# A graph attention layer with q in two float32r pieces and a new cut of the edges into six parts

## The chip, the cores and the metric

One NeuronCore of a Trainium2 chip runs the whole kernel. The metric is the device time of one execution in microseconds. The engines are named as in the profile: PE is the matrix engine (PEld its weight loads), DVE is VectorE, ACT is ScalarE, POOL is GpSimd, SP is SyncE.

## The reference

12,500 nodes with 128 features, 412,500 edges with 64 features. The list `dst` is sorted (it plays the role of the attention's target), `src` is not. Per edge an attention score is made from q of the source, k of the target and the edge's features; a softmax over all edges weighs v of the target, which is summed by source.

```python
h, q, k, v = (x @ W + b for W, b in ((Wn, bn), (Wq, bq), (Wk, bk), (Wv, bv)))
eh = edge_features @ We + be
attn_in = concatenate([q[src], k[tgt], eh], axis=-1)
hmid = leaky_relu(attn_in @ A1 + b1, 0.2)
scores = leaky_relu(hmid @ A2 + b2, 0.2)          # 8 heads
w = softmax(scores.mean(axis=-1), axis=0)         # over all edges
out = segment_sum(w[:, None] * v[tgt], src)
y = layernorm(h + out) * gamma + beta
result = layernorm(x + y)
```

## The kernel before, in words

The edges come in 403 groups of 8 tiles of 128 edges. The groups are cut into six parts (`CUTS`). The nodes are 98 blocks of 128 rows; an edge belongs to the block of its source.

**Making records.** `make(p)` goes through the groups of part p. For a group it loads the edge features and a window of the k and v table, builds one-hots on VectorE (`onehots`, `masked`, `places`: L823 to L883), multiplies them on the matrix engine into a record of 256 numbers per edge (`rows`: L901, L907), copies the records from PSUM on ScalarE (`evacuate`: L918, L919, into a tile `rec` of four times 128 edges, six of them in the pool `rp`), and scatters each 128 edges with an indirect DMA from GpSimd (L930) to the place in `rtab` that is the next free one of the edge's block. Eight scatters per group, 3,224 in all. When a part's last group has been counted, `ended` makes its mask (L967). Each part has its own number of tiles per block, wide enough for the blocks' counts (`plan.tiles`): 5, 6, 7, 7, 7, 7 in the kernel before. Rows of `rtab` that may stay without a record are filled with zeros by DMAs (`fill`, `fill_top`) while the first three parts are made.

**Using records.** A unit is two blocks of one part: 10, 12 or 14 tiles. 49 units a part, 294 in all, 3,822 tiles. For a unit, `load` fetches its records (`rt`), `load_q` its q rows (`qs`), `sources`, `turn`, `turned`, `put`, `spread` bring each edge's row number within its block across all partitions (`sl`, `slT`, `row`, `rowB`). Then come chunks of up to four tiles: `onehot` builds the one-hot `ohT` of a chunk (L1122), `hidden` transposes the record's first half into PSUM (L1133) and adds q by one matmul per piece of q and block (L1142: a chunk that spans two blocks is split in two), `sloped` and `leaky` finish the hidden layer (L1153, L1157). `scores` and `heads` (L1170, L1196) give the scores of the unit, `maximum` (L1217) its running reference, `weights` the exponentials; `select` and `weigh` (L1244, L1258) build weighted one-hots in f32, and `add` (L1287) sums v by source. Sums of a part are added to those of the part before in `atab`.

A planner (`sums_of`) gives each of these calls a step; a unit takes eight steps, also with three chunks, while `e` is 1. The order of the instructions is fixed: while part p is made, the steps of part p - 1 are spread evenly between its groups, from the first load of a part to the first load of the next. Part 0 is made beside the making of the tables (`tables`), the last part's steps run alone after all records are made, and `closing` does the two norms.

**q.** `tables` computes q and h for 14 groups of seven blocks. `parts3` splits q into three bf16 pieces whose sum holds f32's precision (a copy on ScalarE, a difference on VectorE, and so on: L1526, L1531), which lie in `qtab` in DRAM, 768 bytes a row.

Of the kernel before, what the change touches and what calls it, by code (L numbers as in the profile page):

```python
# [11 lines left out]
BF = mybir.dt.bfloat16  # L12
I32 = mybir.dt.int32
# [7 lines left out]
P = 128  # L21
D = 128
# [11 lines left out]
CUTS = 0, 0.1266, 0.2804, 0.4615, 0.6427, 0.8238, 1  # L34
# [9 lines left out]
class Plan:  # L44
# [4 lines left out]
    def __init__(self, n, e, nb, groups):  # L49
        self.n, self.e, self.nb, self.groups = n, e, nb, groups  # L50
        cut = [round(groups * c) for c in CUTS]
# [401 lines left out]
def sorted_path(  # L453
# [17 lines left out]
    qtab = dram.tile([P, nb, 3 * D], BF, name="qtab")  # L471
# [274 lines left out]
    rp = pool("rec", 6)  # L746
# [280 lines left out]
    def sums_of(bp):  # L1027
# [3 lines left out]
        for p, bs, t in units:  # L1031
            nt = len(bs) * t
            nk = -(-nt // 4)
            L, e = 2 * nk, int(nk > 3 or p < NP - 1)
            turn = (11 if nk > 3 else 12) if e else 8
            if plans:
                s0 += 2 * plans[-1][1] if not plans[-1][5] else max(8, 2 * plans[-1][1])


            load_at = free[-BLKS] + 1 if len(free) >= BLKS else 0  # L1040
            lead = turn + 8 if p in starts or p == 0 else turn + 8 + LATE
            s0 = max(s0, load_at + lead - 1)
# [29 lines left out]
        def load_q(i):  # L1072
            bs = units[i][1]
            qs = qp.tile([P, 2, 3, D], BF, name="qs")
            nc.sync.dma_start(
                out=qs[:, : len(bs), :, :].rearrange("p b s d -> p b (s d)"),
# [42 lines left out]
        def onehot(i, t0, n, k):  # L1119
            st = state[i]  # L1120
            st["oh"][k] = op_.tile([P, 4 * P], BF, name="ohT")
# [6 lines left out]
        def hidden(i, t0, c, n, k):  # L1128
# [9 lines left out]
            while j0 < t0 + n:  # L1138
                j1 = min(t0 + n, (j0 // t + 1) * t)
                cols = slice((j0 - t0) * P, (j1 - t0) * P)  # L1140
                for s in range(3):
                    nc.tensor.matmul(  # L1142
                        ph[:, cols], st["qs"][:, j0 // t, s, :], oh[:, cols], start=False,
                        stop=(s == 2 and j1 == t0 + n),
# [389 lines left out]

    def tables():
# [13 lines left out]
        for i, (kv, g) in enumerate(jobs):  # L1549
# [25 lines left out]
            else:  # L1575
                sq = sp.rearrange("p b s t d -> p (b s t d)")[:, : NB * 3 * D].rearrange(
                    "p (b s o d) -> p b s o d", b=NB, s=3, o=1
                )
                yield from parts3([sq[:, :, s, :, :] for s in range(3)], ns[:, :, 0:1, :], 1)
# [153 lines left out]
```

## Time and profile before

| | |
|---|---|
| median of three runs | 5045.82 us (5041.39 to 5046.07) |
| the profiled execution | 5048.47 us, its span 5046.7 us |
| mean granted clock of the matrix engine | 0.909 |
| PE, DVE, ACT, POOL busy | 81%, 81%, 65%, 66% of the span |
| DMA | 1505 MB, 298 GB/s |

A row of a group reads: line, engine, operation, written tile from read tiles, shape, count, then busy time and the mean ns of one, then the idle time of the engine just before them and what ended most of it. A row of stretches reads: from:to, length, then busy time and count of each engine shown, the granted clock of the matrix engine, the DMA engines' busy share, GB/s. A row of waits reads: engine and line, what it waited for, us in total, times, the longest.

### The profile page before, as it was taken

Reading aid. Unit: us, or ns where it says so; the run is one execution under the profiler, and the core shown is the slowest. Engines: PE = TensorE matmul, PEld = TensorE weight load, DVE = VectorE, ACT = ScalarE, POOL = GpSimd, SP = SyncE. Lnnn points to the kernel's source line nnn. Section 1 sums busy time; section 2 is a strip of 40 time slices with the busy share of each in tenths; the row PEclk is TensorE's granted clock in tenths of the full one; section 3 lists DMA queues with packets and bytes.
Section 4 is the critical chain, followed back from the end, with each engine's and each line's share of the span. In section 5 each row is a group of like instructions: output and inputs, shape, how many; then the busy total and the mean of one; then the engine's idle time right before and its main releaser. Section 6 shows DMA issues by size and latency. Waiting matters only on the chain.

```text
span 5046.7 us, 95840 instructions
## 1 busy us (share of the span) xinstructions
PE 4086.8 (81%) x31427; PEld 3042.3 (60%) x31870; DVE 4082.6 (81%) x9078; ACT 3271.6 (65%) x8487; POOL 3318.5 (66%) x3267
## 2 busy tenths in 40 slices
PE   3566667888888888898889899989899999888980
PEld 2333445566666665676667676666676667667760
DVE  7888867778888887888888898888798889666668
ACT  2443345566666666677767777777677777777886
POOL 3777777677777777777777777777777777310002
PEclk6777678899999999999999999999999999999995
DMA  5899889998899988899989899889898999787763
GB/s 179 306 314 354 302 276 335 335 313 292 296 327 329 338 304 288 285 324 318 310 301 316 291 326 317 313 308 311 299 318 311 323 315 325 259 283 271 252 230 140
DMA packets 616624, 1505.35 MB, mean 298 GB/s; under 512 B 104462, under 2 KB 329889, under 8 KB 614324
## 3 DMA queue, kind: packets, MB, share of 16 engines
q1 hardware_dynamic: 461024, 1069.73, 64.1%
q0 software_dynamic: 154752, 429.39, 22.3%
q8 instruction: 253, 4.15, 0.3%
q14 instruction: 255, 2.09, 0.1%
q10 hardware_dynamic: 340, 0.01, 0.0%
HBM read 929.49 MB, written 608.37 MB: 305 GB/s over the span
## 4 chain that ended last, share of the span: by engine, by line
DMA 39%; DVE 24%; PE 11%; POOL 9%; ACT 8%; issue 7%; SPq 1%; DVEq 0%; ACTq 0%; POOLq 0%
DMA rtab<-rec,idx 16%; POOL rtab L930 9%; DMA row<-slT 8%; DMA rt<-rtab 6%; DMA rowB<-row 6%; DVE ohd L844 3%; DVE hm L1157 3%; ACT ohw L1258 3%; PE psm L1287 2%; DVE few L834 2%; ACT rec L918 2%; DVE pos L881 2%; PE pkv L907 2%; DVE ohT L1122 2%; PE psc L1170 1%
## 5 line engine op out<-in xcount | busy, mean ns | idle before, releaser
L930 POOL DMA_INDIRECT rtab<-rec,idx x3224 | 3256.1, 1010 | 1086.1 <-issue 790.7
L918 ACT ACTIVATE rec<-pkv 128x1024 f32<-128x1024 f32 x806 | 822.0, 1020 | 1029.0 <-PE pkv L907 620.2
L1258 ACT ACTIVATE ohw<-ohs,w 128x128 f32<-128x128 bf16 x3822 | 1261.1, 399 | 203.2 <-DVE ohs L1244 84.6
L1287 PE MATMUL psm<-rt,ohw 128*128 128x128 f32 x7644 | 1113.4, 288 | 0.6 <-ACT ohw L1258 0.6
L1287 PEld LDWEIGHTS psm<-rt,ohw 128*128 128x128 f32 x7644 | 985.5, 198 | 75.9 <-ACT hm L1153 10.1
L1157 DVE TENSOR_TENSOR hm<-ph,hm 128x512 f32<-128x512 f32 (+1 forms) x1078 | 669.9, 621 | 271.3 <-ACT hm L1153 263.5
L1133 PE MATMUL ph<-ident,rt 128*128 128x128 f32 x3822 | 648.1, 288 | 154.3 <-DVE hm L1157 150.5
L1142 PE MATMUL ph<-ohT,qs 128*128 128x512 bf16 (+3 forms) x3673 | 719.4, 312 | 35.5 <-DVE ohT L1122 8.9
L901 PE MATMUL pkv<-kvs,ohd 128*128 128x256 bf16 x3224 | 528.7, 290 | 174.2 <-ACT rec L918 153.3
L1133 PEld LDWEIGHTS ph<-ident,rt 128*128 128x128 f32 x3822 | 423.0, 145 | 382.5 <-issue 180.0
L907 PE MATMUL pkv<-WeS,eat 64*128 64x128 f32 x6448 | 626.1, 317 | 0.0
L1122 DVE TENSOR_SCALAR ohT<-rowB,iotaP 128x512 bf16<-128x512 uint8 (+1 forms) x1078 | 499.5, 463 | 152.3 <-DMA rowB<-row 152.1
L1153 ACT ACTIVATE hm<-ph 128x512 f32<-128x512 f32 (+1 forms) x1078 | 577.8, 536 | 57.2 <-PE ph L1142 47.1
L907 PEld LDWEIGHTS pkv<-WeS,eat 64*128 64x128 f32 x6448 | 462.4, 202 | 189.7 <-issue 183.9
L844 DVE TENSOR_SCALAR ohd<-dstb,node 128x1152 bf16<-128x1152 uint8 x404 | 564.9, 1399 | 4.3 <-DMA dstb<-dtab 4.3
L901 PEld LDWEIGHTS <-ohd 128*128 128x128 bf16 x3224 | 314.5, 104 | 379.2 <-issue 289.5
L1142 PEld LDWEIGHTS <-qs 128*128 128x128 bf16 x4116 | 394.8, 99 | 140.6 <-issue 18.6
L1244 DVE TENSOR_TENSOR ohs<-iotaE,sl 128x512 bf16<-128x512 bf16 (+1 forms) x1078 | 419.1, 389 | 4.2 <-ACT ohw L1258 4.2
L834 DVE TENSOR_REDUCE few<-oh 128x99 bf16<-128x792 bf16 x403 | 395.1, 980 | 13.9
L870 DVE TENSOR_TENSOR ats<-pc,oh 128x792 f32<-128x792 f32 x403 | 391.2, 971 | 16.5 <-PE pc L852 16.1
L881 DVE TENSOR_REDUCE pos<-ats 128x8 f32<-128x792 f32 x403 | 389.6, 967 | 1.7
L1170 PE MATMUL psc<-hm,A2s 128*32 128x512 f32 (+3 forms) x2352 | 343.3, 552 | 55.4 <-DVE slT L1101 52.4
(157 smaller groups left out, 3700.6 us busy)
## 6 DMA issues: line engine op xcount, KB each, us to landing
rt<-rtab SPq DMA_DIRECT2D x196, 1820.0 KB
eat<-in_ea SPq DMA_DIRECT2D x201, 512.0 KB
rt<-rtab SPq DMA_DIRECT2D x49, 1560.0 KB
rt<-rtab SPq DMA_DIRECT2D x49, 1300.0 KB
qs<-qtab SPq DMA_DIRECT2D x294, 192.0 KB
rtab<-rec,idx POOLq DMA_INDIRECT x3224
dstb<-dtab SPq DMA_DIRECT2D x201, 256.0 KB
rtab<-empty SPq DMA_DIRECT2D x98, 520.0 KB
```

The costliest lines, as they stand in the source:

```text
L844: nc.vector.tensor_scalar(to, ids[:, cols], node, None, op0=ALU.is_equal)
L901: nc.tensor.matmul(pk[:, h, i, :], ohd[t], kvs, start=(i == 0), stop=False,)
L907: nc.tensor.matmul(pk[:, h, i, :D], eat[h * DE : (h + 1) * DE, (j + i) * P : (j + i + 1) * P], WeS[h * DE : (h + 1) * DE, :], start=False, ...
L918: nc.scalar.activation(rec[:, :, :, : 2 * D], pk, AF.Copy)
L930: one_tile = nc.gpsimd.indirect_dma_start(out=rtab[p % TABS][:, :], out_offset=bass.IndirectOffsetOnAxis(ap=idxs[g][:, t : t + 1], axis=0) ...
L1122: nc.vector.tensor_scalar(st["oh"][k][:, : n * P], st["rowB"][:, t0 * P : (t0 + n) * P], iotaP, None, op0=ALU.is_equal,)
L1133: nc.tensor.matmul(ph[:, j * P : (j + 1) * P], st["rt"][:, t0 + j, :D], ident, is_transpose=True, start=(j == 0), stop=False,)
L1142: nc.tensor.matmul(ph[:, cols], st["qs"][:, j0 // t, s, :], oh[:, cols], start=False, stop=(s == 2 and j1 == t0 + n),)
L1153: nc.scalar.activation(hm, state[i]["ph", k][:, : n * P], AF.Copy, scale=SLOPE)
L1157: nc.vector.tensor_tensor(hm, ph[:, : n * P], hm, op=ALU.max)
L1258: nc.scalar.activation(ohw[:, j, :], ohs[:, :, j], AF.Copy, scale=st["w"][:, t0 + j : t0 + j + 1])
L1287: nc.tensor.matmul(st["psS"][:, (1 + u) * P : (2 + u) * P], ohw[:, j, :], st["rt"][:, t0 + j, D : 2 * D], start=(k == 0), stop=(k == t - 1),)
```

## The change

q is kept as two pieces of four bytes instead of three of two bytes. The first is q as ScalarE writes it in the type float32r, the second the difference to q; `qtab` has 1,024 bytes a row. The one-hot `ohT` is written in float32r too, and `hidden` issues two matmuls per segment instead of three, both operands float32r. In the built program such a matmul stands without a weight load of its own, as f32 ones do; a bf16 one has a separate load. The six parts have 62, 73, 73, 73, 62 and 60 groups (before: 51, 62, 73, 73, 73, 71), which gives 6, 7, 7, 7, 6 and 6 tiles per block. The number of units and of tiles stays (294 and 3,822); the chunks go from 1,078 to 1,029, the q matmuls from 4,116 (1,372 segments of three) to 2,646 (1,323 of two). The block tiles filled with zeros go from 980 to 632. The pool of `rec` has five tiles instead of six. The threshold in `e` moves so that the last part, now with three chunks a unit, keeps its eight steps.

```diff
+FR = mybir.dt.float32r
-CUTS = 0, 0.1266, 0.2804, 0.4615, 0.6427, 0.8238, 1
+CUTS = 0, 62, 135, 208, 281, 343
-        cut = [round(groups * c) for c in CUTS]
+        cut = [groups * c // 403 for c in CUTS] + [groups]
-    qtab = dram.tile([P, nb, 3 * D], BF, name="qtab")
+    qtab = dram.tile([P, nb, 2 * D], FP, name="qtab")
-    rp = pool("rec", 6)
+    rp = pool("rec", 5)
-            L, e = 2 * nk, int(nk > 3 or p < NP - 1)
+            L, e = 2 * nk, int(nk > 2 or p < NP - 1)
-            qs = qp.tile([P, 2, 3, D], BF, name="qs")
+            qs = qp.tile([P, 2, 2, D], FR, name="qs")
-            st["oh"][k] = op_.tile([P, 4 * P], BF, name="ohT")
+            st["oh"][k] = op_.tile([P, 4 * P], FR, name="ohT")
-                for s in range(3):
+                for s in range(2):
                     nc.tensor.matmul(
                         ph[:, cols], st["qs"][:, j0 // t, s, :], oh[:, cols], start=False,
-                        stop=(s == 2 and j1 == t0 + n),
+                        stop=(s == 1 and j1 == t0 + n),
                     )
+    def parts2(to, q):
+        yield
+        nc.scalar.activation(to[:, :, 0, :, :].bitcast(FR), q, AF.Copy)
+        yield
+        yield
+        nc.vector.tensor_tensor(to[:, :, 1, :, :], q, to[:, :, 0, :, :], op=ALU.subtract)
+        yield
+        yield
-                yield from parts3([sq[:, :, s, :, :] for s in range(3)], ns[:, :, 0:1, :], 1)
+                yield from parts2(sq, ns[:, :, 0:1, :])
```

More of the change, by code (lines that the diff above doesn't have):

```diff
@@ L1073, in load_q @@
             bs = units[i][1]
-            qs = qp.tile([P, 2, 3, D], BF, name="qs")
+            qs = qp.tile([P, 2, 2, D], FR, name="qs")
             nc.sync.dma_start(
-                out=qs[:, : len(bs), :, :].rearrange("p b s d -> p b (s d)"),
+                out=qs[:, : len(bs), :, :].rearrange("p b s d -> p b (s d)").bitcast(FP),
                 in_=qtab[:, bs[0] : bs[-1] + 1, :],
@@ L1575, in tables @@
             else:
-                sq = sp.rearrange("p b s t d -> p (b s t d)")[:, : NB * 3 * D].rearrange(
-                    "p (b s o d) -> p b s o d", b=NB, s=3, o=1
-                )
-                yield from parts3([sq[:, :, s, :, :] for s in range(3)], ns[:, :, 0:1, :], 1)
+                sq = sp.rearrange("p b s t d -> p (b s t d)").bitcast(FP)[
+                    :, : NB * 2 * D
+                ].rearrange("p (b s o d) -> p b s o d", b=NB, s=2, o=1)
+                yield from parts2(sq, ns[:, :, 0:1, :])
                 bl = slice(g * NB, (g + 1) * NB)
```

## The prediction

> **What bounds the kernel now.** I read the page's header first, then GpSimd's scatter line (L930) by stretch, then who holds ScalarE up, then the matrix engine's timeline at the end. The stretches are cut where each part's mask is made (L967, the instruction that closes a part): about 622, 1301, 2047, 2815, 3576 and 4322 us.
>
> ```profile
> span 5046.7 us, 95840 instructions
> PE 4086.8 (81%) x31427; PEld 3042.3 (60%) x31870; DVE 4082.6 (81%) x9078; ACT 3271.6 (65%) x8487; POOL 3318.5 (66%) x3267
> ...
> L967 DVE TENSOR_TENSOR mask<-placed,high x6: 659/862/864, 622.2 to 4321.8; 128x686 bf16<-128x686 f32 x4, 128x490 bf16<-128x490 f32 x1, 128x588 bf16<-128x588 f32 x1
> ...
> L930 POOL DMA_INDIRECT rtab<-rec,idx x371 | 406.8, 1097 | 119.8 <-issue 93.9 <-ACT rec L919 7.9 <-DMA rtab<-rec,idx 6.4
> L930 POOL DMA_INDIRECT rtab<-rec,idx x504 | 498.9, 990 | 180.9 <-issue 120.2 <-ACT rec L919 21.0 <-DMA rtab<-rec,idx 9.8
> L930 POOL DMA_INDIRECT rtab<-rec,idx x585 | 583.5, 997 | 178.3 <-issue 145.7 <-DMA rtab<-rec,idx 11.0 <-ACT ohw L1258 5.5
> L930 POOL DMA_INDIRECT rtab<-rec,idx x571 | 572.5, 1003 | 174.1 <-issue 136.5 <-ACT ohw L1258 11.6 <-DMA rtab<-rec,idx 6.4
> ...
> 3582.05 0.96 POOL L930 DMA_INDIRECT rtab<-rec,idx  x1 [0.31 <-issue]
> 3583.32 0.96 POOL L930 DMA_INDIRECT rtab<-rec,idx  x1 [0.30 <-issue]
> 3584.59 0.96 POOL L930 DMA_INDIRECT rtab<-rec,idx  x1 [0.30 <-issue]
> ```
>
> The header makes GpSimd look idle a third of the time. The L930 rows (stretches 97:622, 622:1301, 2815:3576, 3576:4322) say otherwise. In 2815:3576, 585 scatters of 0.997 us, each behind 178.3/585 = 0.305 us of idle time, fill 761.8 of 761 us. The three timeline rows show the same beat: one scatter every 1.27 us, idle time 0.30 us without a cause outside GpSimd. So from the third part on GpSimd issues scatters without a break, and a group of 1,024 edges (8 scatters) takes 10.42 us whatever the other engines do. Until 4322 us the kernel is a scatter generator; only the end, when no records are made any more, belongs to the others.
>
> How close are the others behind? The waits of ScalarE tell, for 2815:3576 and for 3576:4322:
>
> ```profile
> ACT rec L918 <- DMA rtab<-rec,idx: 105.6, 56, 3.7
> ...
> ACT rec L918 <- PE pkv L907: 91.8, 60, 5.6
> ...
> L1287 PE MATMUL psm<-rt,ohw 128*128 128x128 f32 x7644 | 1113.4, 288 | 0.6 <-ACT ohw L1258 0.6
> 2815.00:3576.00 761.00, 199.79 (x1374) 176.03 (x1373) 0.97 0.90 312
> 3576.00:4322.00 746.00, 201.69 (x1384) 176.80 (x1383) 0.97 0.90 312
> 4322.00:4907.00 585.00, 212.11 (x1532) 194.13 (x1532) 0.98 0.75 256
> 4907.00:5047.00 140.00, 0.00 (x0) 0.00 (x0) 0.52 0.43 161
> ```
>
> In the first of the two stretches ScalarE stood 105.6 us because all `rec` buffers were still with GpSimd: slack. In the second its largest wait is for the matrix engine's next record. L1287 has two records a tile, so its windows count tiles: 687 tiles over 73 groups (9.4 a group) with slack, 692 over 71 (9.75 a group) with next to none, while GpSimd still never starved. So 9.75 tiles a group is the point where the two loads balance. The last two rows give the end: 766 tiles in 585 us without groups (0.764 us a tile), then 140 us of norms.
>
> Is that end bound by the matrix engine? One steady unit of 14 tiles there:
>
> ```profile
> 4700.32 1.06 PE L1287 MATMUL psm<-rt,ohw 128*128 128x128 f32 x8
> ...
> 4702.30 0.38 PE L1217 MATMUL psm<-ident,mx 128*128 128x128 f32 x2
> 4702.52 1.06 PE L1287 MATMUL psm<-rt,ohw 128*128 128x128 f32 x8
> 4703.51 1.06 PE L1170 MATMUL psc<-hm,A2s 128*32 128x512 f32 x8
> 4704.50 0.66 PE L1133 MATMUL ph<-ident,rt 128*128 128x128 f32 x4
> 4704.99 0.82 PE L1142 MATMUL ph<-ohT,qs 128*128 128x384 bf16 x6
> 4705.65 0.66 PE L1287 MATMUL psm<-rt,ohw 128*128 128x128 f32 x4
> 4706.15 0.60 PE L1133 MATMUL ph<-ident,rt 128*128 128x128 f32 x4
> 4706.58 0.81 PE L1142 MATMUL ph<-ohT,qs 128*128 128x512 bf16 x3
> 4707.23 1.05 PE L1287 MATMUL psm<-rt,ohw 128*128 128x128 f32 x8
> 4708.12 0.95 PE L1196 MATMUL psm<-headsum,z 128*128 128x4 f32 x8
> 4709.00 0.22 PE L1094 MATMUL psc<-identB,sl 128*14 128x128 bf16 x1
> 4709.15 0.44 PE L1133 MATMUL ph<-ident,rt 128*128 128x128 f32 x2
> 4709.43 0.49 PE L1142 MATMUL ph<-ohT,qs 128*128 128x256 bf16 x3
> 4709.76 0.50 PE L1287 MATMUL psm<-rt,ohw 128*128 128x128 f32 x3
> ```
>
> No gap stands in these rows: yes. From 4700.32 to 4709.76 a unit takes 9.44 us. Taken start to start, the q matmuls (L1142) are 0.65 for a full chunk of 512 columns in three pieces (4706.58 to 4707.23), the same for the other (4700.32 to 4702.30 is 0.89 of L1287, 0.43 of L1133 and the rest), 0.66 for the chunk split 384+128, 0.33 for 256: 2.29 us.
>
> **The change, term by term.** *The cuts.* 403 groups and 3,224 scatters stay, at GpSimd's beat, so moving groups between parts costs nothing in itself; the six parts come to 6, 7, 7, 7, 6, 6 tiles a block in place of 5, 6, 7, 7, 7, 7 (3,822 tiles in both). The end now belongs to a part of 6 tiles. Of its 766 tiles 686 are the last part's; at 12 tiles a unit in place of 14 it has 766 x 12/14 = 657, in the same 54.7 units. Price of a 12-tile unit: from 9.44 take q (2.29), the turn (0.15), the maximum (0.22), heads (0.88) and scores (0.99): 4.91 us over 14 tiles, 0.351 each. So 12 x 0.351 = 4.21, plus 0.15, 0.22, 3/4 of heads (0.66) and of scores (0.74): 5.98 without q.
>
> *q in two pieces.* A 12-tile unit has chunks 512, 256+256, 512: with three bf16 pieces 2 x 0.65 + 2 x 0.33 = 1.96 us. The trace has no float32r matmul. Ends: a bf16 piece, 0.65/3 = 0.22 us per 512 columns, and an f32 one (L1287: two records a tile, four tiles from 4707.23 to 4708.12, 0.22 us per 128 columns), four times as much. I take the lower: the two f32 records are what carries 24 bits of mantissa, and a type whose one piece falls short of that, so that q needs two, should have no second record. That is an inference, and the middle, one record at the spacing of the single f32 record (L1133, 0.43 us for four of 128 columns, twice bf16), is a rival below. So two thirds: 1.31 us, a unit of 7.29 us; 2.29 becomes 1.53 in a 14-tile unit, 0.76 less.
>
> ```profile
> L1142 PEld LDWEIGHTS <-qs 128*128 128x128 bf16 x4116 | 394.8, 99 | 140.6 <-issue 18.6
> L1133 PEld LDWEIGHTS ph<-ident,rt 128*128 128x128 f32 x3822 | 423.0, 145 | 382.5 <-issue 180.0 <-DVE hm L1157 149.3 <-PE psm L1287 9.6
> ```
>
> Against this change speaks a rule of the Trainium skill ("TensorE: Matmul & The Clock Gate", Weight-path perf modes): the fast weight load is on for types other than FP32. The trace agrees in kind: a bf16 weight load took 99 ns, an f32 one 145 ns. By that page's figure for a plain load (its section on LDWEIGHTS: columns over 1.2 GHz, so an estimate of 0.107 us) a piece of 128 columns would take 0.107 in place of 0.054 us; the 12-tile units have none, the fifth part's units two each, 49 x 2 x 0.053 = 5 us, and the sum would be 4972.
>
> *The end.* 54.7 units at 9.44 are 516 of the 585 us; the other 69 are DMA waits early in it:
>
> ```profile
> DVE ohT L1122 <- DMA rowB<-row: 93.3, 43, 4.3
> DVE sl L1086 <- DMA rt<-rtab: 77.6, 46, 15.5
> ```
>
> These stay. 54.7 x 7.29 + 69 = 468; since units follow each other faster than loads used to, I add 12 (0 to 25): 480 us in place of 585. The 140 us behind it stay.
>
> *What the cuts take back.* While the fifth part is made (62 groups), the fourth part's 686 tiles are worked off: 11.06 tiles a group, 1.31 over the balance of 9.75. At 9.44/14 = 0.674 us a tile that is 0.88 us a group, at 0.764 it is 1.00; two-piece q gives back 49 x 0.76/62 = 0.60. So 0.28 to 0.40 a group over the beat, 17 to 25 us; I take 24, as no slack was left there. In the sixth (60 groups, some 600 tiles, 10.0 a group) 0.17 more against 49 x 0.65/60 = 0.53 less: nothing.
>
> *Five `rec` buffers.* A buffer is four scatters, 5.1 us of cover for GpSimd. In the middle parts ScalarE waits for buffers, so cover is spare; where a part ends a dip of up to one buffer may starve GpSimd: 0 to 5 x 5.1 = 25, I take 8.
>
> *The one-hot in 4 bytes.*
>
> ```profile
> L1122 DVE TENSOR_SCALAR ohT<-rowB,iotaP 128x512 bf16<-128x512 uint8 x833 | 409.8, 492 | 152.3 <-DMA rowB<-row 152.1
> L1122 DVE TENSOR_SCALAR ohT<-rowB,iotaP 128x256 bf16<-128x256 uint8 x245 | 89.7, 366 | 0.0
> L1157 DVE TENSOR_TENSOR hm<-ph,hm 128x512 f32<-128x512 f32 x833 | 569.4, 684 | 217.6 <-ACT hm L1153 212.6 <-ACT ohw L1258 3.7
> ```
>
> 256 more columns cost 126 ns, two elements a nanosecond. With f32 output it is between 492 and L1157's 684 ns; the source stays one byte, so I take 492. At 684, 49 x 3.5 x 0.19 = 33 us of VectorE a part, of which the crowded fifth might show half.
>
> *Tables and fills.* q's two pieces save one ScalarE and one VectorE pass a block group in part 0, where nobody waits for them (GpSimd's beat). Of 980 block tiles of empty rows 632 remain. In 97:622 a scatter took 1.097 us against 1.003 later, 371 x 0.094 = 35 us lost to crowded queues; I take 6 off, 0 to 17. qs loads grow by a third (192 KB each), beside work.
>
> *Sum.* 4322 - 6 + 24 + 8 + 480 + 140 = 4968 of span; the profiled execution took 5048.5 us for its span of 5046.7, and is 2.7 over the median of 5045.8. So 4967 us, 1.6% faster. A step of 0.2% (10 us) is about what a measurement of this kernel can tell.
>
> **The rivals.** *Two float32r pieces cost as much as three bf16* (0.17). Then a unit is 7.94 us, the end 515 with the same 12; the fifth part is 0.88 to 1.00 a group over the beat, 54 to 62; sum 4322 - 6 + 58 + 8 + 515 + 140 - 1 = 5036, between 5000 and 5085. For it: only 4-byte rows slower than bf16 are in the trace.
>
> *The matrix engine becomes the bound* (0.16): one record a piece, but at twice bf16's spacing, as L1133. Two pieces then cost 4/3 of three: 2.61 in a 12-tile unit (8.59 us), 3.05 in a 14-tile one, 0.76 more. The fifth part is over its beat by 0.94 + 0.60 = 1.54 a group, 95 us; the sixth by 0.17 + 0.53 = 0.70, 42; the third and fourth use up their slack and lose some 10 each; the end is 551. Sum 4322 - 6 + 95 + 42 + 20 + 8 + 551 + 140 - 1 = 5171. It turns slower than before once two pieces cost over some 1.03 times what three do. At L1287's full f32 price it would be hundreds more. Against: the inference above.
>
> *Cover lost* (0.05): `rec` with five and a 4-byte one-hot at 684 ns starve GpSimd through the last three parts, 25 + 3 x 17: about 5035.
>
> **How the numbers follow.** The forecast has 0.62; its own range is 4912 (no giving back, all of the fills' gain, 468 at the end) to 5005. With the first rival up to 5060 some 0.8 is held. Faster: 0.61 of the forecast, 0.10 of the first rival, 0.02 of the last; within 10 us 0.05; slower the second rival and 0.06 of the others.
>
> **What would show it.** Right: scatters still 1.27 us apart through the third and fourth part; L1142 two records a segment, 0.43 us a full chunk start to start; first gaps of GpSimd behind `rec` in the fifth part; last mask near 4350; some 480 us from there to the last L1287; norms 140. Wrong: gaps of GpSimd in every part (cover), L1142 at 0.65 us or more a chunk (price), or an end that waits for `rt` and `rowB` instead of the matrix engine.

## The result and the profile after

The changed kernel takes 5081.92 us (median of five runs, 5072.5 to 5090.75) where the kernel before takes 5045.13 in the same session: a ratio of 1.0072, 95% interval 1.006 to 1.0084. It is slower by 37 us, 0.7%; the forecast was 4967, faster by 79, with a range of its own up to 5005 and up to 5060 with the first rival's.

The page's header after, the line that closes a part (its six times run from the first to the last part's end), and the stretches cut at those times, in the columns of the prediction:

```profile
span 5085.8 us, 92648 instructions
...
L968 DVE TENSOR_TENSOR mask<-placed,high x6: 760/834/864, 721.7 to 4394.5; 128x588 bf16<-128x588 f32 x3, 128x686 bf16<-128x686 f32 x3
...
2248.00:3011.00 763.00, 680.72 (x5383) 533.48 (x5383) 660.49 (x1427) 555.09 (x1469) 584.90 (x585) 0.95 0.91 316
3011.00:3734.00 723.00, 645.31 (x5084) 508.95 (x5083) 606.63 (x1353) 530.64 (x1418) 506.09 (x508) 0.95 0.90 310
3734.00:4395.00 661.00, 579.13 (x4644) 440.15 (x4643) 563.68 (x1223) 457.21 (x1256) 477.86 (x482) 0.96 0.90 311
4395.00:4947.00 552.00, 468.78 (x3257) 380.16 (x3256) 310.59 (x924) 350.44 (x1083) 33.77 (x19) 0.91 0.71 245
4947.00:5086.00 139.00, 0.00 (x0) 0.00 (x0) 118.32 (x550) 84.12 (x224) 29.00 (x14) 0.50 0.45 168
```

The ledger, from these cuts and those of before. After 281 groups the changed kernel stands at 3011; the kernel before reached group 281 at about 2815 + 22 x 10.42 = 3044. So it is **33 us ahead** there. From then on before needed 1277 us for 122 groups, 10.47 each. The fifth part (62 groups) took 723 us where that beat gives 649: **74 lost**. The sixth (60 groups) took 661 for 628: **32 lost**. The end took 552 for 585: **32 won**, where 105 were forecast. The norms took 139 for 140. In all 39 us of span, which is the 5085.8 against 5046.7.

The mask that closes a part is VectorE's, and it can come before GpSimd has sent the part's last records. So the same ledger was taken at GpSimd's scatters, counted in the two traces. The changed kernel is 15 us ahead after 62 groups, 39 after 135 and 38 after 281; the next 62 groups lose 68, the last 60 lose 25. The last scatter comes at 4345 before and at 4400 after, the first load of the last part's records right behind it (4347 and 4403). Before, the last mask stood 23 us ahead of that scatter, after it only 5. From that first load to the last L1287 the 49 units of the last part took 559 us before and 544 after: of the 32 us won at the end by the masks, only 15 belong to the smaller units.

GpSimd's scatter line in the second, the fifth and the sixth part (722:1483, 3011:3734, 3734:4395):

```profile
L931 POOL DMA_INDIRECT rtab<-rec,idx x588 | 583.0, 991 | 179.2 <-issue 146.3 <-DMA rtab<-rec,idx 10.7 <-ACT ohw L1259 4.6
L931 POOL DMA_INDIRECT rtab<-rec,idx x508 | 507.1, 998 | 217.2 <-issue 116.4 <-ACT rec L920 27.4 <-ACT w L1236 18.5
L931 POOL DMA_INDIRECT rtab<-rec,idx x482 | 478.4, 993 | 183.4 <-issue 114.6 <-ACT rec L920 24.3 <-ACT ohw L1259 12.8
```

In the second part the idle time before a scatter is 179.2/588 = 0.305 us, the beat. Before it was 180.9/504 = 0.359 there: the old second part, with 62 groups beside units of 10 tiles, had been starved, and the new one with 73 beside 12 is not. By the beat, this cost the kernel before 679 - 62 x 10.42 = 33 us, as much as the lead at 281 groups. In the fifth part the idle time is 0.428, in the sixth 0.380, and ScalarE's `rec` stands among the causes: the groups now wait for something else.

The q matmuls of full chunks, the one-hot, and the q matmuls' weight loads (before: 492 ns a one-hot, 99 ns a weight load); then the weight loads of `add` in the kernel before:

```profile
L1143 PE MATMUL ph<-ohT,qs 128*128 128x512 f32 x1176 | 437.5, 454 | 0.0
L1123 DVE TENSOR_SCALAR ohT<-rowB,iotaP 128x512 fp32r<-128x512 uint8 x882 | 430.9, 489 | 100.5 <-DMA rowB<-row 100.1
L1143 PEld LDWEIGHTS ph<-ohT,qs 128*128 128x128 f32 x2646 | 411.1, 197 | 15.5 <-DVE ohT L1123 15.0
...
L1287 PEld LDWEIGHTS psm<-rt,ohw 128*128 128x128 f32 x7644 | 985.5, 198 | 75.9 <-ACT hm L1153 10.1 <-issue 7.8 <-ACT ohw L1258 7.7
```

The records name the type f32, but there is one record a piece (1176 = 2 x 588 full chunks), as the forecast inferred; what grew is the weight load, 197 ns for 99. The rule of the Trainium skill that the prediction weighed ("TensorE: Matmul & The Clock Gate", Weight-path perf modes) agrees in kind, but not in size: the page's figure gave an estimate of 0.107 us a load, the trace has 0.197. The prediction charged it to the split chunks alone, 5 us. The trace before had a nearer price: the f32 loads of L1287 took 198 ns there, and the 145 ns quoted for f32 are those of the transposes (L1133).

One unit at the end after, first on the matrix engine, then SyncE's issues (SPq in the rows) in the same stretch:

```profile
4702.69 0.66 PE L1134 MATMUL ph<-ident,rt 128*128 128x128 f32 x4 [1.64 <-DVE hm L1158]
4703.10 0.71 PE L1143 MATMUL ph<-ohT,qs 128*128 128x512 f32 x2
4703.74 0.22 PE L1095 MATMUL psc<-identB,sl 128*12 128x128 bf16 x1
...
4707.29 0.71 PE L1143 MATMUL ph<-ohT,qs 128*128 128x512 f32 x2
4707.84 0.60 PE L1134 MATMUL ph<-ident,rt 128*128 128x128 f32 x4
4708.19 0.72 PE L1143 MATMUL ph<-ohT,qs 128*128 128x256 f32 x4
4708.75 1.05 PE L1288 MATMUL psm<-rt,ohw 128*128 128x128 f32 x8
...
4711.53 0.66 PE L1134 MATMUL ph<-ident,rt 128*128 128x128 f32 x4 [1.15 <-DVE hm L1158]
```

```profile
4702.37 0.39 SPq L1065 DMA_DIRECT2D rt<-rtab  x1
4704.96 0.31 SPq L1109 DMA_DIRECT2D row<-slT  x1
...
4710.48 0.32 SPq L1114 DMA_DIRECT2D rowB<-row  x1
...
4711.85 0.40 SPq L1065 DMA_DIRECT2D rt<-rtab  x1
```

A chunk in two pieces takes 0.64 us start to start (4703.10), 0.55 (4707.29) and 0.56 when split in halves (4708.19): 1.75 a unit, where three bf16 pieces were put at 1.96 and the forecast at 1.31. And the matrix engine, with 7.7 us of work in this unit, stands between units. SyncE shows why: `row` is issued 2.6 us behind the load `rt` of 1,560 KB, `rowB` can go only when `row` has landed, 5.5 us later, and the next `rt` stands behind `rowB` in SyncE's stream, 9.5 us after the one before. The granted clock was 0.91 in the end after and 0.98 before (the stretch rows); how much of the busy time that makes was not separated. The waits over the end say the same of all units: VectorE's and SyncE's of after (4400:4940), then SyncE's of before (4400:4890).

```profile
DVE sl L1087 <- DMA rt<-rtab: 128.2, 49, 5.1
DVE ohT L1123 <- DMA rowB<-row: 53.6, 45, 2.4
...
SPq L1114 <- DMA row<-slT: 258.8, 51, 8.2
...
SPq L1113 <- DMA row<-slT: 158.4, 45, 5.5
```

Before, VectorE's wait for `rt` was 77.6 us in 46 times; now it is 128.2 in 49. What the matrix engine saved went for the most part into waiting for loads.

### The profile page after: what moved, and what is told of

Its sections match the earlier page's. It is cut to its first block, busy times and chain, and to the rows that moved or that the text cites. A ratio compares the mean times of both kernels' runs of the same rounds, so it can differ in the third digit from the quotient of the medians.

```text
span 5085.8 us, 92648 instructions
## 1 busy us (share of the span) xinstructions
PE 4044.1 (80%) x30302; PEld 3083.9 (61%) x30302; DVE 4049.9 (80%) x8917; ACT 3162.5 (62%) x8312; POOL 3305.8 (65%) x3266
## 4 chain that ended last, share of the span: by engine, by line
DMA 31%; DVE 19%; PE 10%; ACT 10%; POOL 9%; issue 7%; SPq 1%; DVEq 0%; ACTq 0%; POOLq 0%
DMA rtab<-rec,idx 15%; POOL rtab L931 9%; DMA rt<-rtab 9%; DMA row<-slT 5%; ACT ohw L1259 4%; DVE ohd L845 3%; DVE hm L1158 3%; PE psm L1288 3%; DMA rowB<-row 2%; ACT rec L919 2%; DVE few L835 2%; ACT hm L1154 2%; PE pkv L908 2%; DVE pos L882 1%; DVE ohT L1123 1%
## 5 line engine op out<-in xcount | busy, mean ns | idle before, releaser
L1288 PE MATMUL psm<-rt,ohw 128*128 128x128 f32 x7644 | 1151.9, 296 | 3.2 <-ACT ohw L1259 3.2
L1288 PEld LDWEIGHTS psm<-rt,ohw 128*128 128x128 f32 x7644 | 1022.5, 205 | 59.9 <-ACT hm L1154 9.9
L1158 DVE TENSOR_TENSOR hm<-ph,hm 128x512 f32<-128x512 f32 (+1 forms) x1029 | 662.5, 644 | 349.5 <-ACT hm L1154 343.4
L902 PE MATMUL pkv<-kvs,ohd 128*128 128x256 bf16 x3224 | 544.9, 297 | 344.6 <-ACT rec L919 320.3
L1143 PE MATMUL ph<-ohT,qs 128*128 128x512 f32 (+3 forms) x2646 | 733.6, 377 | 10.1 <-DVE ohT L1123 10.1
L908 PE MATMUL pkv<-WeS,eat 64*128 64x128 f32 x6448 | 645.0, 324 | 0.0
L908 PEld LDWEIGHTS pkv<-WeS,eat 64*128 64x128 f32 x6448 | 476.8, 208 | 197.1 <-issue 189.2
L1123 DVE TENSOR_SCALAR ohT<-rowB,iotaP 128x512 fp32r<-128x512 uint8 (+1 forms) x1029 | 485.9, 472 | 100.5 <-DMA rowB<-row 100.1
L1143 PEld LDWEIGHTS ph<-ohT,qs 128*128 128x128 f32 x2646 | 411.1, 197 | 15.5 <-DVE ohT L1123 15.0
L1245 DVE TENSOR_TENSOR ohs<-iotaE,sl 128x512 bf16<-128x512 bf16 (+1 forms) x1029 | 407.6, 396 | 1.5 <-ACT ohw L1259 1.5
L1171 PE MATMUL psc<-hm,A2s 128*32 128x384 f32 (+2 forms) x2352 | 336.0, 556 | 35.9 <-DVE slT L1102 27.0
```

Of the source, the lines that this page charges most:

```text
L902: nc.tensor.matmul(pk[:, h, i, :], ohd[t], kvs, start=(i == 0), stop=False,)
L908: nc.tensor.matmul(pk[:, h, i, :D], eat[h * DE : (h + 1) * DE, (j + i) * P : (j + i + 1) * P], WeS[h * DE : (h + 1) * DE, :], start=False, ...
L1123: nc.vector.tensor_scalar(st["oh"][k][:, : n * P], st["rowB"][:, t0 * P : (t0 + n) * P], iotaP, None, op0=ALU.is_equal,)
L1143: nc.tensor.matmul(ph[:, cols], st["qs"][:, j0 // t, s, :], oh[:, cols], start=False, stop=(s == 1 and j1 == t0 + n),)
L1158: nc.vector.tensor_tensor(hm, ph[:, : n * P], hm, op=ALU.max)
L1288: nc.tensor.matmul(st["psS"][:, (1 + u) * P : (2 + u) * P], ohw[:, j, :], st["rt"][:, t0 + j, D : 2 * D], start=(k == 0), stop=(k == t - 1),)
```

## The experiments

Each is compared with the kernel before on its own chip in the same session (that one moved between 5045 and 5063 us). e6 to e9, e12, e16 and e17 are one execution each, the others four to twelve. Where the expectations name theories: A holds that the price of the q pieces makes it slower, C that the loads of the units do.

**Which part of the change costs.** e1 has the new cuts with q as before (three bf16 pieces, `rec` with six tiles), e2 the new q with the old cuts.

```diff
e1  -    qtab = dram.tile([P, nb, 2 * D], FP, name="qtab")
    +    qtab = dram.tile([P, nb, 3 * D], BF, name="qtab")
    -    rp = pool("rec", 5)
    +    rp = pool("rec", 6)
    ... (qs, ohT, hidden and parts3 as before)
e2  -CUTS = 0, 62, 135, 208, 281, 343
    +CUTS = 0, 0.1266, 0.2804, 0.4615, 0.6427, 0.8238, 1
    ... (the cut and e's threshold as before)
```

> The new cuts alone: q in three bf16 pieces, six rec buffers. Theory A (two float32r pieces cost the matrix engine nearly what three bf16 ones do, 0.55 to 0.64 us a full chunk in the trace of the changed kernel, so the parts with 11.06 and 10.0 tiles a group fall behind GpSimd's beat): the last mask near 4395 to 4415, the end (last mask to last L1287) near 550, total 5075 to 5105. Rival (the sixth rec buffer was the cover that is missing): the fifth and sixth parts keep 10.4 to 10.6 us a group, the last mask near 4300, total near 4985.

> The old cuts with q in two float32r pieces and five rec buffers. Theory A: no part has over 9.75 tiles a group, so making keeps GpSimd's beat within 15 us (last mask 4310 to 4335), the end is bound by its loads and stays 575 to 590, total 5030 to 5055. Rival (rec buffers, or the price of float32r alone): the last mask moves past 4360, total above 5080.

e1: 1.0067 (1.0053 to 1.0081), e2: 1.0015 (1.0006 to 1.0024), with 5059 us just above the 5055 at which its expectation ended. The cuts are nearly the whole loss. With three bf16 pieces and six `rec` tiles the fifth part takes 728 us, the sixth 662, the end 545, as after, so neither the q pieces nor the fifth `rec` tile causes them. With the old cuts the new q gives an end of 580 us for 585: cheaper matmuls alone win some 5 there, and lose more before it (last mask 4337 for 4322).

**Is it an engine?** e3 has the new cuts and adds only two of the three bf16 pieces; e6 leaves out VectorE's maximum (L1158, 0.68 us a chunk).

```diff
e3 (on e1)      -                for s in range(3):
                +                for s in range(2):
e6 (on after)   -            nc.vector.tensor_tensor(hm, ph[:, : n * P], hm, op=ALU.max)
```

> The new cuts, six rec buffers, and only two of q's three bf16 pieces are multiplied (the third is left out): the price that the prediction took for float32r, 0.43 us a full chunk. Theory A: the fifth and sixth parts lose only 15 to 40 us to the beat, last mask near 4310 to 4345. Theory B on the end (a loop through the DMA queue: the next rt load is issued only after rowB, rowB waits for row, and row stands behind the present rt load in the same queue): the end stays 540 to 555, total 5000 to 5040. Rival (the end is bound by the matrix engine): the end falls to some 480, total near 4950.

> The changed kernel without VectorE's maximum in the hidden layer (L1158 of its trace, 0.68 us a chunk; it is left out). Rival V: the fifth and sixth parts speed up by most of 49 x 2.4 = 118 us each until GpSimd's beat holds them: 11.7 and 11.0 us a group become 10.4 to 10.7, the last mask near 4300 to 4320. Theory C: VectorE was not what they waited for; they stay above 11.2 and 10.8, the end above 530.

The fifth part, the sixth and the end in e3, then in e6:

```profile
3013.00:3737.00 724.00, 635.73 (x5019) 489.30 (x5086) 606.80 (x1353) 530.28 (x1418) 510.70 (x510) 0.94 0.88 306
3737.00:4399.00 662.00, 573.79 (x4586) 431.08 (x4640) 562.71 (x1223) 457.29 (x1255) 477.37 (x483) 0.95 0.90 306
4399.00:4942.00 543.00, 456.36 (x3206) 357.86 (x3257) 310.99 (x926) 350.68 (x1084) 34.12 (x19) 0.92 0.70 243
...
3008.00:3733.00 725.00, 650.36 (x5093) 517.36 (x5093) 508.11 (x1162) 530.51 (x1421) 503.78 (x507) 0.92 0.89 310
4387.00:4940.00 553.00, 455.70 (x3275) 365.54 (x3273) 217.79 (x766) 352.39 (x1090) 36.67 (x22) 0.94 0.71 246
```

e3 has the q matmuls at the forecast's own price, and still the fifth part takes 724 us, the end 543, the kernel 1.007 (1.0054 to 1.0087). Theory A, which expected the last mask at 4310 to 4345 (it came at 4399), falls: had the price been right, the result would have been the same. e6 takes some 100 us off VectorE in the fifth part (606.6 to 508.1) and the part stays at 725 (5081 in all, one run). Neither engine sets these stretches.

**Is it the loads?** e7 leaves out the loads of the edges' features (256 KB a group); in e8 the last part's units load half of their records; in e9 all units from the fourth part on do.

```diff
e7  -                eat = eap.tile([P, 2, EG // 2], FP)
    -                nc.sync.dma_start(out=eat[:, :m, :], in_=ea[:, g : g + m, :])
    +                eat = eat0
    +                if g == 0:
    +                    nc.sync.dma_start(out=eat[:, :m, :], in_=ea[:, g : g + m, :])
e8  +            h = t // 2 if p == NP - 1 else t
    -                out=rt[:, :n, :].rearrange("p (u t) w -> p u (t w)", u=m),
    +                out=rt[:, : m * h, :].rearrange("p (u t) w -> p u (t w)", u=m),
    ... (the loaded half is read twice)
e9  +            if p >= 3:
    +                n, m = t, 1
    ... (the first block's records are read for both)
```

> The changed kernel with the edge features loaded for the first two groups alone (all other groups use those; 201 loads of 512 KB are left out): relief for the DMA queue in the making parts, none for the engines. Theory C: rt lands sooner (issue to use 11.0 us before), the fifth and sixth parts go to 10.4 to 11.0 us a group, last mask 4310 to 4365; the end is unchanged (545 to 560). Rival V: 11.5 to 11.8 and 10.9 to 11.1 a group as before, last mask near 4390.

> The changed kernel, where each unit of the last part loads the records of six tiles instead of twelve and uses each twice (half of the records are left out): all instructions stay, the rt load has half its bytes. Theory C: rt to use falls from 7.9 to 4 to 5.5 us, the end from 552 to 440 to 490 us (the matrix engine's 7.7 us a unit then bounds it), total 4975 to 5025. Rival V: the end stays 535 to 560.

> The changed kernel, but the units of the fourth part and of those behind it load only their first block's records and use them for both blocks, so the second block's records are left out of the result. The same instructions run on all engines; half of the record bytes go from the DMA queues while the fifth and the sixth part are made and at the end. Theory C (the units' loads are what keeps a unit at 14.6 us in the fifth part and at 10.3 us at the end): the fifth part falls from 723 us to 650 to 680, the sixth from 660 to 625 to 640, the last mask comes at 4290 to 4330 in place of 4394, the end is about 470. Rival (the engines' own coupling while groups and units run together): the fifth part stays at 700 us or more, the sixth at 640 or more, the last mask comes behind 4360; the end is about 470 all the same.

The fifth part in e7; the end in e8; in e9 the fifth, the sixth part and the end, and GpSimd's line in the fifth:

```profile
3005.00:3709.00 704.00, 642.43 (x5091) 507.76 (x5091) 606.64 (x1356) 530.59 (x1418) 509.10 (x506) 0.95 0.88 296
...
4385.00:4856.00 471.00, 440.74 (x3257) 350.54 (x3256) 318.83 (x922) 347.37 (x1083) 34.33 (x19) 0.99 0.65 204
...
3019.00:3684.00 665.00, 618.68 (x5081) 492.12 (x5079) 604.99 (x1351) 527.90 (x1418) 510.73 (x506) 0.98 0.84 271
3684.00:4312.00 628.00, 567.53 (x4644) 433.20 (x4643) 561.73 (x1223) 454.69 (x1255) 473.91 (x476) 0.99 0.82 264
4312.00:4788.00 476.00, 442.62 (x3260) 351.80 (x3258) 318.61 (x925) 347.85 (x1085) 41.51 (x26) 0.99 0.63 202
...
L931 POOL DMA_INDIRECT rtab<-rec,idx x506 | 511.6, 1011 | 154.6 <-issue 115.5 <-ACT ohw L1268 11.0 <-DMA rtab<-rec,idx 8.8
```

e9 runs the same instructions on every engine with fewer bytes: the sixth part is at the beat (628 us for 60 groups), the fifth at 665 (0.306 us of idle time a scatter), the end at 476, the kernel at 4929 (one run). That is about the forecast's timetable (4967, an end of 480): what holds the changed kernel back, and what the forecast lacked, is the load of the records. The DMA share falls from 0.90 to 0.84 there. In e8 the end, 471 us, has the matrix engine busy 440.7 of them. That both ends come near the 480 is luck in part: in e8 a steady unit takes 8.48 us, with 0.4 us of waiting on the matrix engine, where 7.29 was forecast, and the 69 and 12 us of waits that the forecast added are nearly gone.

e7 takes 16 MB from the fifth part (62 x 256 KB) and 20 us go, the end stays at 554; the kernel is at 5044. The part is at 11.3 us a group, between its two expectations. At the 310 GB/s of after the 16 MB would be worth 52 us; instead the rate fell to 296.

**Is it the bytes or the way through SyncE's queue?** In e12 the units worked off in the fifth and the sixth part send `row` and `rowB` through ScalarE's queue. e16 and e17 go the other way, on the kernel before: in its fifth part, which runs at GpSimd's beat, the edges' features move twice, in e16 into the same buffer, in e17 to a place in DRAM that nothing waits for.

```diff
e12 -            nc.sync.dma_start(out=st["row"][:nt, :], in_=st.pop("slT")[:nt, :])
    +            queue = nc.scalar if units[i][0] in (3, 4) else nc.sync
    +            queue.dma_start(out=st["row"][:nt, :], in_=st.pop("slT")[:nt, :])
    ... (the same for rowB)
e16 +                for _ in range(2 if p == 4 else 1):
                         nc.sync.dma_start(out=eat[:, :m, :], in_=ea[:, g : g + m, :])
e17 +                if p == 4:
    +                    nc.sync.dma_start(out=dbl[:, :m, :], in_=ea[:, g : g + m, :])
```

> The changed kernel, but the units of the fourth and the fifth part (those worked off while the fifth and the sixth part are made) send row and rowB through ScalarE's hardware queue in place of SyncE's; the same bytes, the same steps. If the bytes set the pace of these parts (310 GB/s at a busy share of 0.90), the fifth part stays at 710 to 730 us and the sixth at 650 to 670. If the chain of row and rowB in SyncE's queue does, they fall by 20 us or more each, to 700 or less and 640 or less, and the last mask comes before 4355 in place of 4394.

> The kernel before; in its fifth part alone (73 groups, 761 us at GpSimd's beat, 312 GB/s) the edge features are loaded twice into the same buffer, 19 MB more. If the DMA engines are at their ceiling there at 312 GB/s, these 19 MB take 61 us: the part goes to 800 to 830 us with gaps between the scatters, and the other parts stay. If there is room (a bound that lies in the units' own chain of steps and not in bytes), the part stays at 761 to 775 us, at 330 GB/s or more.

> The kernel before; in its fifth part alone (73 groups, 761 us at GpSimd's beat, 312 GB/s) the edge features are also copied from DRAM to a scratch place in DRAM, once for two groups, 19 MB in all, and nothing waits for these copies. If the DMA engines are at their ceiling, the 19 MB at 312 GB/s take 61 us: the part goes to 800 to 830 us with gaps between the scatters at 305 to 320 GB/s. If there is room, the part stays at 761 to 775 us, at 330 GB/s or more.

The fifth part in e12; SyncE's largest wait around e16's fifth part (2900:3650); e17's fifth part, and SyncE's wait for `row` in it (2900:3600), then in before (2900:3500); last, two stretches of 100 us of before:

```profile
3024.00:3759.00 735.00, 650.86 (x5088) 508.52 (x5086) 608.13 (x1354) 529.12 (x1417) 507.32 (x505) 0.95 0.89 306
...
SPq L796 <- DMA eat<-in_ea: 222.9, 31, 13.1
...
2820.00:3625.00 805.00, 704.90 (x5622) 528.52 (x5621) 661.48 (x1425) 561.44 (x1475) 602.32 (x602) 0.94 0.92 322
...
SPq L1116 <- DMA row<-slT: 190.6, 41, 8.7
...
SPq L1113 <- DMA row<-slT: 127.9, 39, 6.2
...
400.00:500.00 100.00, 60.20 (x298) 38.90 (x297) 80.65 (x136) 33.59 (x51) 77.50 (x73) 0.70 1.03 349
...
1600.00:1700.00 100.00, 84.71 (x653) 62.53 (x660) 83.27 (x170) 63.22 (x170) 76.42 (x78) 0.95 0.99 337
```

e12 makes it worse (735 us, and 683 for the sixth part; 5139 in all), outside both of its expectations. SyncE's wait for `row` moves to ScalarE there, so the run shows that this move does not help, not that the wait is harmless. e16 missed its aim: its fifth part took 884 us, but SyncE stood 223 us for the first copy to land before it could issue the second into the same buffer, so the run shows what a wait in SyncE's stream costs, not what bytes do.

e17 is cleaner: no instruction waits for its 19 MB. They stretch the part from 761 to 805 us, at 322 GB/s and a DMA share of 0.92 where before had 312 and 0.90. At 312 GB/s they would have cost 61 us, with free room nothing; they cost 44 by the masks, and by GpSimd's scatters 26 in the part's 73 groups and 38 up to the last one. So more loading costs time there, but neither e17 nor e7 pays the price of a fixed rate. The copies also went through SyncE's queue, and `row` landed later behind them: SyncE waited 190.6/41 = 4.6 us for it, 127.9/39 = 3.3 in before. Bytes and order in the queue are not separated by these runs.

Nor is a share of 0.90 full by itself: in before, GpSimd kept its beat from 1600 to 1700 (78 scatters) at 0.99 and 337 GB/s, and 400:500 had 1.03 and 349, with other transfers in the mix (the fills). (The Trainium skill, "DMA: Bandwidth & Descriptors", Specifications, gives about 358 GB/s as a core's limit to HBM; none of the stretches shown here reached it, but slices of 8 us between 300 and 620 of before did, up to 389.)

**Can the end be loosened?** Five runs. In e4 the last part's `row` and `rowB` go through GpSimd's software queue, in e5 through ScalarE's hardware queue. e10 adds to e5 that the steps before them come one or two earlier; e11 is e10's edit on the kernel before; e13 is e11 with `turn` left in place.

```diff
e4  +            queue = nc.gpsimd if units[i][0] == NP - 1 else nc.sync
e5  +            queue = nc.scalar if units[i][0] == NP - 1 else nc.sync
e10, e11 (e5's queue, and for the last part)
    +                do(s0 - turn_at - 1, turn, i)
    +                do(s0 - turn_at, turned, i)
    +                do(s0 - turn_at, put, i)
    +                do(s0 - turn_at + 3, spread, i)
e13 (e5's queue, and for the last part, g = 1)
    +            do(s0 - turn_at + 1 + e - g, turned, i)
    +            do(s0 - turn_at + 1 + e - g, put, i)
    +            do(s0 - turn_at + 3 + 2 * e - g, spread, i)
```

> The changed kernel, with the last part's two small transfers (row and rowB) issued by GpSimd on its own queue, and so no longer behind rt. Theory B: rt loads of several units are in flight, VectorE's wait for rt falls from 128 to under 40 us, the end goes from 552 to 430 to 490 us (the matrix engine's own work is some 7.7 us a unit), total 4960 to 5020; making is unchanged (last mask near 4395). Rival (the end is bound by the matrix engine, or by the chain maximum, reference, weights): the end stays above 535, total above 5065.

> The changed kernel, with the last part's row and rowB issued by ScalarE on its own hardware queue. After e4 (GpSimd's queue: VectorE's wait for rt went from 127 to 13 us, but row to ohT took 10 us a unit, and the end grew) the question is what a unit of the end waits for. Theory C (a unit costs the DMA round of rt, row and rowB, nearly the same with 12 as with 14 tiles): with both small transfers past rt and not slowed by software descriptors the end falls from 552 to 440 to 510 us, total 4990 to 5045. Rival V (the units' pace is VectorE's, or its chain with ScalarE): the end stays 540 to 560, total 5070 to 5095.

> The changed kernel with two edits for the last part's units alone: row and rowB go through ScalarE's hardware queue in place of SyncE's, and turn, turned, put and spread come one or two steps earlier. Theory C (at the end two loops through the loads set the pace, the record load behind the row and the row behind the record load): with both loosened the end falls from 552 us to 440 to 510 and the kernel to 4975 to 5040. Rival (the record load alone takes 10 us a unit beside the row's and rowB's transfers, whatever their queue and step): the end stays above 540 and the kernel at 5070 to 5095.

> The kernel before with the same two edits, for its last part of 14 tiles a unit. Theory C: the end falls from 585 us to 510 to 550, the kernel to 4975 to 5015. Rival (the record load itself): the end stays above 570, the kernel within 15 us of 5045.

> The kernel before; for the last part's units alone row and rowB go through ScalarE's hardware queue, and turned, put and spread come one step earlier, while turn stays at its step. If e11's end (604 us for 585) was lost to the turn, which had been put right behind the activation of the heads, this end is 545 to 575 us and the kernel 5005 to 5035. If the 10.7 us of a unit of 14 tiles are the matrix engine's own with the engines around it, the end stays at 580 to 605 and the kernel at 5040 to 5065.

| | end, us | ratio to before (95%) |
|---|---|---|
| after | 552 | 1.0072 (1.006 to 1.0084) |
| e4 | 565 | 1.01 (1.0085 to 1.0114) |
| e5 | 556 | 1.0078 (1.0061 to 1.0095) |
| e10 | 515 | 1.001 (0.9997 to 1.0022) |
| before | 585 | 1 |
| e11 | 604 | 1.0022 (1.0013 to 1.003) |
| e13 | 599 | 1.0028 (1.0017 to 1.004) |

The end in e10, VectorE's waits there, and VectorE's and ScalarE's waits in e11 (4450:4850):

```profile
4384.00:4899.00 515.00, 484.24 (x3259) 372.02 (x3257) 313.83 (x925) 352.61 (x1084) 34.03 (x19) 0.98 0.77 263
...
DVE hm L1160 <- ACT hm L1156: 158.2, 136, 2.8
DVE ohT L1125 <- DMA rowB<-row: 17.7, 16, 1.9
DVE sl L1087 <- DMA rt<-rtab: 12.3, 11, 3.7
...
DVE hm L1159 <- ACT hm L1155: 143.6, 143, 2.8
...
ACT ohw L1260 <- DMA row<-slT: 29.8, 10, 3.4
```

e4 and e5 take the wait of the record load away (128 to some 17 us on VectorE) and win nothing, against what theories B and C expected; VectorE's wait for `rowB` grows instead, from 54 to 103 us in e5 and 117 in e4 (4400:4940 and 4400:4960). Only with both loosened does the end give: e10 wins 37 us of it, and the kernel comes out even with the one before, not faster. (The profiled execution of e10, 5039 us, is the fastest of its ten, whose median is 5058; by the ratios e10 wins some 31 us over after.) The end stays above the 440 to 510 that were expected.

On the kernel before the same edit cost 19, though VectorE no longer waits for `rt`. So in the kernel before the loads are not shown to be what holds the end. VectorE waits 144 us for ScalarE there, but that is no reason: in e10, which wins, it waits 158. ScalarE itself stands 30 us for `row` before it can issue `rowB`. Putting `turn` back (e13) did not mend it, so its step was not the reason; an end of 599 us is what e13's second reading, a unit bound by the engines, expected.

**Can the old cuts be bettered by the same reading?** e14 moves three groups to the old second part, the starved one, from parts with slack; e15 adds e13's edit.

```diff
-CUTS = 0, 0.1266, 0.2804, 0.4615, 0.6427, 0.8238, 1
+CUTS = 0, 51, 116, 188, 260, 332
-        cut = [round(groups * c) for c in CUTS]
+        cut = [groups * c // 403 for c in CUTS] + [groups]
```

> The kernel before with parts of 51, 65, 72, 72, 72 and 71 groups (before: 51, 62, 73, 73, 73, 71): the second part, which stands beside units of 10 tiles and was starved at 10.9 us a group, gets three groups more, which three parts with slack give up. If bytes or units and not groups set the second part's time, it stays at 680 to 700 us with its 65 groups, the last mask comes at 4290 to 4312 in place of 4322, and the kernel at 5010 to 5035. If a group more costs its 10.4 us there as well, or the second part's seventh tile a block costs as much in fills and loads, the last mask stays at 4317 to 4330 and the kernel within 10 us of before.

> The edits of the two runs before this one together. Their gains lie in different stretches, so they should add up: 4975 to 5020 us if both are there, within 15 us of before if neither is.

The first and the second part in e14, then the first of before:

```profile
97.00:659.00 562.00, 318.95 (x1609) 203.40 (x1609) 437.62 (x695) 204.02 (x270) 405.39 (x371) 0.70 0.94 324
659.00:1361.00 702.00, 560.00 (x4270) 402.03 (x4315) 530.43 (x1134) 399.49 (x1049) 514.25 (x525) 0.87 0.90 303
...
97.00:622.00 525.00, 316.86 (x1608) 203.39 (x1608) 437.32 (x694) 203.89 (x270) 405.46 (x371) 0.70 0.94 322
```

Both expectations fail on the slow side: e14 1.0092 (1.0075 to 1.0109), e15 1.0118 (1.01 to 1.0136). With 65 groups the second part needs seven tiles a block; the fills for its wider blocks fall into the first part, which does the same 371 scatters with the DMA engines as full as before, moves 13 MB more (562 x 324 against 525 x 322) and ends 37 us later. The second part took 702 us, 10.8 a group where it had been 10.95, so the three groups cost nearly what the others do; whether by their bytes or by the 49 units beside them was not separated. The last mask comes at 4379 for 4322. No version that does the whole computation beats the kernel before.

## Why the prediction was wrong

**The bound of the making stages** was read as GpSimd's beat with the engines' work behind it, "9.75 tiles a group is the point where the two loads balance". The beat was right and held through the fourth part after, 1.27 us a scatter. The second bound was wrong: not tiles on an engine (e3, e6) but the loads of the units' records (e9). The rows quoted for it had a DMA share of 0.90 and 312 GB/s in both stretches; I read the matrix engine's count in them and left the DMA engines out of the sum. How bytes would have priced it: while before made its fifth part, 73 groups and 49 units of 14 tiles moved 761 x 312 GB/s, 237 MB; a group alone is some 1.52 MB (the sizes in the page's list of DMA transfers: scatters 1.07, edge features 0.26, the rest 0.20). Eleven groups fewer are 221 MB, at 312 GB/s 707 us, against a beat of 646; measured are 723 at 310, 224 MB. That comes near, but it is an estimate, and e7 and e17 do not keep to a fixed rate.

**The term "What the cuts take back"**, 24 us with nothing for the sixth part, is the first that failed: 74 and 32 were measured by the masks, 68 and 25 by the scatters. Estimated by bytes as above it would have been some 60 for the fifth alone.

**The end** is the second, 480 us for a measured 552. The 9.44 us of a unit are a true period: L1217 stands at 4702.30, 4711.73 and 4721.17. But it is the period of units that do not wait, fewer than half of the last part's (the next L1217 comes at 4731.78, 10.6 us on). L1217 has two records a unit, and its group over 4400:4890 of before and of after (L1218) gives the mean:

```profile
L1217 PE MATMUL psm<-ident,mx 128*128 128x128 f32 x92 | 17.9, 277 | 0.0
...
L1218 PE MATMUL psm<-ident,mx 128*128 128x128 f32 x94 | 22.3, 326 | 0.3 <-DVE mx L1212 0.3
```

490/46 = 10.65 us a unit before, 490/47 = 10.43 after. The missing 1.2 us were put down as "DMA waits early in it", a sum of 69 us that would stay, with 12 more, whatever the matrix engine does; but 43 and 46 waits in some 55 units are nearly one a unit. In the changed kernel that sum did not stay. A unit with less work on the matrix engine waits longer, because the loop through `rt`, `row` and `rowB` sets its period: with half of the records loaded the same units take 8.48 us (e8), with queue and steps of the small transfers changed the end falls to 515 (e10). The prediction named "an end that waits for `rt` and `rowB`" as a sign against it, and that is what came. Whether the end of the kernel before is held by the same loop is open, since e11 and e13 did not shorten it.

**The price of float32r** was also off: 1.75 us a unit where 1.31 was taken and 1.96 would be no gain (part of it may be the clock of 0.91: in e8, at 0.99, a chunk takes 0.56 in the median, 1.68 a unit). The inference (one record a piece) held; the weight load of 98 ns more was not counted. The rival "two pieces cost as much as three" is thus the nearer on price, but its 5036 was wrong too, since e3 shows that the price decides nothing here.

**Cuts and fills early on** were put at 6 us won, and 33 were: "moving groups between parts costs nothing in itself" missed that the old second part was starved, which its row (idle 180.9 for 504) showed. What the fills did was not separated. By the lists of DMA transfers the block tiles filled with zeros are 686 before and 534 after, not 980 and 632; in the first part they rise from 392 to 436, in the second they fall from 196 to 98. **`rec`** with five tiles was put at 8 and costs nothing that e1 against after can show. **The one-hot** in four bytes, 492 ns forecast, is 489. **The norms** and the scatter beat were right.

In sum 4968 was forecast and 5085.8 measured: 46 from the last mask (4394.5 for 4348), 72 from the end.

**Open:** in e7 gaps remain at 0.88 and 296 GB/s, so there is no one sharp ceiling, and how far the in-order queues set the pace of the making parts was not separated from the bytes. A cost per unit is not excluded either: the starved parts (62 groups before; 62 and 60 after) all have fewer groups beside their 49 units than those at the beat (71 to 73), and only e9 touches that, through the loads. Why e11 and e13 lose while e10 wins is not known.

## What to carry to other kernels

Before moving work between stages, read the DMA share and GB/s of each stage beside the engines, and what the transfers of a stage wait for: a stage at GpSimd's beat can have a second bound close behind it that no engine's waits name, and a stage with fewer groups beside the same loads runs into it. Take the period of a pipelined loop over many turns and not from one that has no gap, and count its waits: as many as turns means that they belong to the loop and will not stay the same when the work in it shrinks. When a stage is cut at one engine's instruction, see where the other engines stand at that moment. When a wait goes through one in-order queue, removing it alone may only show the next wait of equal length.

## What the runs showed of the hardware

A float32r matmul here leaves one record a piece and 197 ns of weight load, where bf16 has 99 and f32 198 (L1287) or, for transposes, 145 (L1133); 512 columns in two pieces took 0.55 to 0.64 us, three bf16 pieces 0.65. VectorE writes the one-hot in float32r as fast as in bf16 (489 and 492 ns). After a `row` of 1.5 KB issued 2.6 us behind a record load of 1,560 KB in the same queue, `rowB` could go only 5.5 us later. A wait of 7 us on average in SyncE's stream (e16, 223 us in 31 times) went with a part 123 us longer, where e17 with as many bytes and without the wait had 44.
